# Queries of the narrow-headed cross attention made tile by tile amid its steps, and rooms for returned rows allotted first

## The chip, the cores and the metric

The kernel runs on one core of one Trainium2 chip. The metric is the device time of one execution in microseconds, as the median of several runs. The page and the trace come from one profiled execution. Its engines are PE (matrix products, with PEld for its weight loads), DVE (vector), ACT (scalar), POOL (GpSimd) and SP, which here issues DMAs. "PEclk" or "granted clock" is the share of full speed that PE's clock had.

## The reference, cut to what matters

A network of four levels works on x, 16 batches of 64 rows of 256 numbers (1024 rows, 8 tiles of 128), with a context of 16 x 1024 rows of 192. Every level adds a cross attention to the context, an attention of some kind and an expert or dense layer. All numbers are f32. The change touches the cross attention of level 1 and, at its edge, the expert layer of level 0 ahead of it:

```python
# L0_ffn: 8 experts, two for each row
y = sum over e of comb[:, e] * swiglu(x_e, w1[e], w2[e], w3[e])   # + a shared swiglu
# L1_xattn: 16 heads of 16, on the normalised x
q = (x @ Wq.T + bq).reshape(b, l, 16, 16)
kv = (y @ Wkv.T + bkv).reshape(b, m, 16, 32); k, v = kv[..., :16], kv[..., 16:]
att = softmax(einsum('blhd,bmhd->blmh', q, k) / 4, axis=2)
out = einsum('blmh,bmhd->blhd', att, v).reshape(b, l, 256) @ Wo.T + bo
...
x = x + L0_ffn(layernorm(x))
x = x + L1_xattn(layernorm(x), ctx)
```

## The kernel before, in words

One program runs eight stages one after the other: L0_first, L0_ffn, L1_xattn, L1_attn, L1_ffn, L2_xattn_attn, L2_ffn and L3. x stays in SBUF as `xs`, eight tiles of 128 rows by 256. The order of PE's instructions is written out by hand in each stage. The orders of the other engines are set by a scheduler from the same code, so work of a later stage can stand amid that of an earlier one on DVE, ACT and POOL, and PE's order may do so at a stage's edge. Each stage has an SBUF pool (`self.lp`) at one end of memory, with the stages taking turns between the two ends; a tile of a new stage that lies on tiles of an old one waits until those tiles' last readers are done. PSUM of L1_xattn has three banks tagged `misc` (L69), used in turn.

**End of L0_ffn.** Expert results were written to DRAM (`ys`). For each of 8 tiles and each of two experts, `take_back` (L1191) gathers 128 rows by an indirect DMA on POOL's queue (L1189) into a room tagged `back` with three buffers, and DVE adds them, weighed, to `xs` (L1102): 16 gathers and 16 adds.

**L1_xattn** (L782 to L966). It begins by setting up small masks (L795 on) and its tile `qs`, two versions of all queries, 16 KB a partition each: `qs0` as computed and `qs1` with its two halves of 64 partitions exchanged, by DMA (L826). Then, in PE's order:

1. `keys_values(0)` (L830): four pieces, keys(0), values(0), keys(1) and values(1), for batch 0. Keys take four passes of 512 columns over 128 rows (L844) and four over 64 (L846), into two banks that DVE (L849) and ACT (L850) evict with a bias into `kT`. Values take eight passes (L858) and eight (L865), evicted into `v` by DVE (L58) and ACT (L60).
2. `biases()` (L806): the output bias and that of the values as one row of 256, spread over 128 partitions. DVE makes `bv` (L809), PE multiplies, and ACT copies to `bias` (L812).
3. `norm_x()` (L182): normalises all eight tiles. Per tile DVE takes statistics (L152, L154, L156), POOL the power -0.5 (`ln_rs`, L158), DVE writes `htok` (L168), PE transposes twice (L177) and an eviction writes into `hT` (L58 or L60).
4. Eight additions of `bias` to `xs` on POOL (L934).
5. `queries(0)` and `queries(1)` (L814): 16 passes of 512 columns, eight DVE operations of 128x512 (L821) that add a bias and mask the two heads of a pair, and four DMAs of 512 KB.
6. 64 steps (L937 on), four for each batch. A step makes scores (L65, `sc<-kT,qs`, two versions of `qs` for the two halves of keys), on which DVE takes row maxima (L221) and ACT exponentials (L223). Beside them PE does a quarter of the next batch's keys or values, transposes the exponentials of the step before (L233, evicted by DVE at L237 and ACT at L235) and multiplies them by values (L892). Every eight steps a tile's result is weighed, projected and added to `xs` (L85).

Of the kernel before, what the change touches and what calls it, by code (L numbers as in the profile page):

```python
# [10 lines left out]
F32 = mybir.dt.float32  # L11
# [3 lines left out]
ALU = mybir.AluOpType  # L15
# [3 lines left out]
B, S, D = 16, 64, 256  # L19
T = B * S  # L20
NT = T // 128
# [19 lines left out]
class Net:  # L41
# [740 lines left out]
    def L1_xattn(self):  # L782
# [4 lines left out]
        nc = self.nc  # L787
        wq, wk, wv, wo, bo = self.pack()
# [7 lines left out]
        for h in range(2):  # L796
            nc.sync.dma_start(sels[0][32 * h : 32 * h + 8], sel[:, h])
            for half in range(2):
                at = 64 * half
                nc.sync.dma_start(sels[1][32 * h : 32 * h + 8, :, at : at + 64], sel[:, h, :, 64 - at : 128 - at])  # L800

        qs = [self.lp.tile([128, 2, B, 2, S], F32, name=f"qs{n}") for n in range(2)]

        bias = self.lp.tile([128, D], F32, name="bias")

        def biases():  # L806
            bv = self.lp.tile([128, 2, 128], F32, name="bv")
            for c in range(2):
                nc.vector.tensor_scalar(bv[:, c, :], self.ones, self.col("L1x_bv", c), None, ALU.mult)  # L809
            ps = self.misc([128, D])  # L810
            self.mm(ps, [(bv[:, c, :], wo[:, c, :]) for c in range(2)] + [(self.ones[:1, :], bo)])
            nc.scalar.copy(bias, ps)  # L812

        def queries(half):  # L814
            cols = bass.ts(half, 512)
            bs = slice(half * 8, half * 8 + 8)
            for o in range(2):
                ps = self.misc([128, 512])
                self.mm(ps, [(wq[:, c, o * 128 : (o + 1) * 128], self.hT[:, c, cols]) for c in range(2)])
                for h in range(2):  # L820
                    nc.vector.tensor_scalar(  # L821
                        qs[0][:, o, bs, h, :], ps.rearrange("p (b s) -> p b s", s=S),
                        self.col("L1x_bq", o), self.pair4[:, h : h + 1], ALU.add, ALU.mult,
                    )
            for r in range(2):
                nc.sync.dma_start(qs[1][64 * r : 64 * r + 64, :, bs], qs[0][64 - 64 * r : 128 - 64 * r, :, bs])  # L826

        kv = {}

# [44 lines left out]
        def scores(b, g, sums):  # L874
            kT = kv[b][0]
            sc = [self.lps.tile([128, KEYS], F32, tag="sc", bufs=2, name="sc") for _ in range(2)]
            c = g // 2
            for kh in range(2):
                at = bass.ts(kh, 512)
                for u in range(2):  # L880
                    j = (2 * g + u + 2 * kh) % 4
                    rows = slice(32 * j, 32 * j + 32)
                    self.mm(sc[u][:, at], [(qs[kh][rows, c, b].rearrange("p h q -> p (h q)"), kT[rows, c, at])])
            return [self.exp_rows(sc[u], sums[:, 2 * g + u : 2 * g + u + 1]) for u in range(2)]

        def averages(b, g, pT, o):
# [39 lines left out]

        self.room_t = self.misc
        with self.tc.manual_schedule(engines={mybir.EngineType.PE}):
            for piece in keys_values(0):
                piece()  # L930
            biases()
            self.norm_x()
            for i in range(NT):
                nc.gpsimd.tensor_tensor(self.xs[:, i, :], self.xs[:, i, :], bias, ALU.add)  # L934
            for half in range(2):
                queries(half)
            held, work = None, {}  # L937
            steps = [(b, g) for b in range(B) for g in range(4)]
            for k in range(len(steps) + 4):
                now, pT = None, []  # L940
                if held is not None:
                    hb, hg, p, hs = held
                    for u in range(2):
                        pT.append(self.keys_first(p[u]))
                if k < len(steps):
                    b, g = steps[k]
                    if not g:
                        sums = self.lp.tile([128, 8], F32, tag="sums", bufs=3, name="sums")
                        more = keys_values(b + 1) if b + 1 < B else None
                    now = (b, g, scores(b, g, sums), sums)  # L950
                for piece in work.pop((k, "early"), ()):
                    piece()
                if k < len(steps):
                    if more is not None:
                        more[g]()
                if held is not None:
                    if not hg:
                        o = self.lps.tile([128, 2, 2, 128], F32, tag="o", bufs=1, name="o")
                    averages(hb, hg, pT, o)
                for piece in work.pop((k, "late"), ()):  # L960
                    piece()
                if held is not None and hg == 3:
                    i, par = hb // 2, hb % 2
                    if not par:
                        ym = self.lp.tile([128, 2, 2, 2, S], F32, tag="ym", bufs=2, name="ym")
                    own_columns(o, ym, par)  # L966
                    work[k + 1, "early"] = [lambda hs=hs, par=par, rT=rTs[i % 2]: shares(hs, par, rT)]
                    if par:
                        work[k + 2, "early"] = [lambda ym=ym, rT=rTs[i % 2]: weigh(ym, rT)]
                        work[k + 3, "late"] = [lambda i=i, ym=ym: project(i, ym)]  # L970
                held = now
# [83 lines left out]

    def L0_ffn(self):
        nc = self.nc
        p = self.gate_softmax(self.logits)
        masks, both = self.two_largest(p)
        self.scattered = []  # L1060
        place, count = self.ranks(both)
        first, self.rows = self.blocks(count, L0_BLOCKS)
        at, gates = [], []
        for k, m in enumerate(masks):
            at.append(self.slots_of(m, place, first, f"s{k}"))
            self.scatter(at[k], "L0f")
            g = self.gate("g_of")
            nc.vector.tensor_tensor(g, p, m, ALU.mult)
            gates.append(self.over_experts(g, ALU.add, f"g_{k}")[0])
        for _ in self.swiglu(  # L1070
            *self.shared, 384, self.add_to_x, 1, lambda: self.lps.tile([128, 512], F32, tag="gu", bufs=4, name="gu")
        ):
            pass
        self.start_pack(self.at)
        sizes = [128] * 5 + [64]
        for j in range(L0_BLOCKS):
            w13, w2 = self.L0_block(j)
            dT = self.block_tokens(j)
            hid = self.lp.tile([128, 6, 128], F32, tag="hid1", bufs=2, name="hid1")
            for m2 in range(3):  # L1080
                ps = self.lps.tile([128, 2, 2, 128], F32, tag="gu", bufs=4, name="gu")
                for v in range(2):
                    m = m2 * 2 + v
                    n = sizes[m]
                    for u in range(2):
                        self.mm(
                            ps[:n, u, v, :], [(w13[:, u, c, m * 128 : m * 128 + n], dT[:, c, :]) for c in range(2)]
                        )

                for lo, v, n in ((0, 2, 128),) if m2 < 2 else ((0, 1, 128), (1, 1, 64)):  # L1090
                    g = self.lp.tile([128, 2, 128], F32, tag="g1", bufs=3, name="g1")
                    nc.scalar.activation(g[:n, :v, :], ps[:n, 0, lo : lo + v, :], AF.Silu)
                    nc.vector.tensor_tensor(
                        hid[:n, m2 * 2 + lo : m2 * 2 + lo + v, :], g[:n, :v, :], ps[:n, 1, lo : lo + v, :], ALU.mult
                    )
            po = self.lps.tile([128, D], F32, tag="o", bufs=2, name="po")
            self.mm(po, [(hid[:n, m, :], w2[:n, m, :]) for m, n in enumerate(sizes)])
            self.block_out(j, po)
        for i in range(NT):
            for k in range(2):  # L1100
                y = self.take_back(at[k], i)
                nc.vector.scalar_tensor_tensor(  # L1102
                    self.xs[:, i, :], y, gates[k][:, i : i + 1], self.xs[:, i, :], ALU.mult, ALU.add
                )
# [85 lines left out]

    def take_back(self, at, i):  # L1191

        y = self.lp.tile([128, D], F32, tag="back", bufs=3, name="back")
        self.gather_rows(y, self.ys, at[:, i : i + 1])
        return y

    def block_tokens(self, j):

# [28 lines left out]
    def L1_ffn(self):  # L1227
        nc = self.nc
        rw, rb, b2 = self.pack()
        self.norm_x()  # L1230
        p = self.gate_softmax(self.gate_logits(rw, rb))
        mask = self.first_largest(p, "t1")
# [16 lines left out]
        for j in range(L1_BLOCKS):  # L1249
# [3 lines left out]
            for m4 in range(2):  # L1253
                ph = self.lps.tile([128, 4, 128], F32, tag="h", bufs=3, name="ph")
                for u in range(4):
                    m = m4 * 4 + u
# [26 lines left out]
    def L2_ffn(self):  # L1283
        nc = self.nc
        gw, gb = self.pack()
        self.norm_x()
        lg = self.gate("lg")
        nc.vector.tensor_copy(lg, self.gate_logits(gw, gb))
# [903 lines left out]
```

## Time and profile before

| what | us |
|---|---|
| runs | 3138.62, 3132.53, 3132.1 |
| median | 3132.53 |
| profiled execution | 3130.54 |
| its span in the trace | 3128.8 |
| first gather of returned rows, start | 542.11 |
| last L1102 add, start | 570.83 |
| PE's first pass after it (keys(1) of batch 0) | 572.20 |
| first half of scores of step 0 | 592.04 |
| second half of scores of step 0 | 597.48 |
| scores of step 1 | 607.11 |
| scores of step 2 | 614.26 |

The span is 1.7 us shorter than the profiled execution that it belongs to, and that execution is 2 us shorter than the median of the runs. Times of the table's lower part count from the span's start. A step's length can be read from the last two rows: 7.15 us. In the stretches of the profile, a row gives an interval, its length, then for each engine the busy time with its instruction count in brackets, the granted clock, the DMA engines' mean busy share and GB/s. In a timeline, brackets at the end of a line give the idle time of that engine just before and what ended it.

### The profile page before, as it was taken

What the parts mean: (1) busy time and instruction counts of PE and PEld (TensorE: products, weight loads), DVE (VectorE), ACT (ScalarE), POOL (GpSimd) and SP (SyncE); (2) the same over time, 40 slices, a digit from 0 to 9 for tenths busy, and PEclk for the clock granted to TensorE, in tenths of its full rate; (3) what the DMA queues carried; (4) which work ended last, traced back from release to release, by engine and by line L of the source; (5) the groups of instructions that cost most, each with busy time, mean ns of one, the idle gap of its engine ahead of it and who ended that gap; (6) DMA issues with size and microseconds to landing.
All of it is one profiled execution on the core that took longest, in us unless ns stands there. A gap on an engine that the chain in (4) does not pass through costs nothing.

```text
span 3128.8 us, 42567 instructions
## 1 busy us (share of the span) xinstructions
PE 2750.3 (88%) x16976; PEld 1987.6 (64%) x16976; DVE 1463.2 (47%) x2986; ACT 1010.6 (32%) x2160; POOL 310.5 (10%) x425
## 2 busy tenths in 40 slices
PE   6887899699999879788999999496999888887899
PEld 3654787366666536675777776494777566665668
DVE  2553111566666672124444443322345656658591
ACT  1221121255555411122322332021225445455330
POOL 1112221200000010320011000202000000000000
PEclk9897899799999988799999999698999999998999
DMA  9612774201010100761211111373113212122110
GB/s 231 187 41 73 276 275 179 60 31 32 21 32 23 47 1 27 271 217 35 60 42 41 52 51 51 126 248 112 51 41 87 70 41 88 47 72 58 52 37 7
DMA packets 149408, 273.18 MB, mean 87 GB/s; under 512 B 16511, under 2 KB 103258, under 8 KB 142426
## 3 DMA queue, kind: packets, MB, share of 16 engines
q1 hardware_dynamic: 127418, 170.90, 18.6%
q0 software_dynamic: 14784, 93.26, 8.3%
q10 hardware_dynamic: 7008, 6.29, 0.6%
q8 instruction: 134, 2.20, 0.3%
q14 instruction: 64, 0.52, 0.1%
HBM read 247.83 MB, written 20.45 MB: 86 GB/s over the span
## 4 chain that ended last, share of the span: by engine, by line
PE 65%; DVE 10%; issue 7%; ACT 4%; DMA 3%; POOL 2%; SPq 1%; ACTq 0%; DVEq 0%; POOLq 0%
PE misc L65 10%; PE sc L498 8%; PE halves L65 7%; PE gu L65 6%; PE po L65 4%; PE misc L233 4%; PE ps_h L65 4%; PE ps_t L233 3%; PE sc L65 2%; PE misc L844 2%; PE o L892 2%; PE misc L858 2%; DVE x L1832 2%; ACT p L223 2%; PE misc L177 2%
## 5 line engine op out<-in xcount | busy, mean ns | idle before, releaser
L221 DVE TENSOR_REDUCE nmx<-sc 128x1 f32<-128x1024 f32 x264 | 311.7, 1219 | 243.9 <-PE sc L498 148.1
L223 ACT ACTIVATE p<-sc,nmx 128x1024 f32<-128x1024 f32 x264 | 294.0, 1115 | 323.7 <-DVE nmx L221 322.4
L498 PE MATMUL sc<-ctxT,qp 128*128 128x512 f32 (+1 forms) x1024 | 353.9, 600 | 0.0
L498 PEld LDWEIGHTS sc<-ctxT,qp 128*128 128x128 f32 (+1 forms) x1024 | 138.2, 189 | 153.4 <-issue 151.9
L158 POOL TENSOR_TENSOR ln_rs<-ln_ve,nhalf 128x1 f32<-128x1 f32 x120 | 66.7, 561 | 1531.3 <-DVE ln_ve L156 1267.0
L65 PE MATMUL halves<-ctx,pT 128*128 128x193 f32 x1024 | 189.3, 339 | 9.2 <-DVE xs L85 4.1
L65 PEld LDWEIGHTS halves<-ctx,pT 128*128 128x128 f32 x1024 | 177.2, 200 | 12.0 <-DVE xs L85 4.6
L65 PE MATMUL misc<-ctx,pT 128*128 128x193 f32 x1024 | 179.3, 327 | 0.9 <-DVE qT L463 0.9
L65 PEld LDWEIGHTS misc<-ctx,pT 128*128 128x128 f32 x1024 | 167.7, 191 | 2.8 <-DVE qT L463 1.6
L233 PE MATMUL ps_t<-ident,p 128*128 128x128 f32 x1088 | 148.0, 279 | 18.1 <-ACT p L223 10.5
L1832 DVE TENSOR_TENSOR_SCAN x<-da,x 128x512 f32<-128x512 f32 x128 | 152.2, 1213 | 2.1 <-ACT da L1822 1.4
L235 ACT COPY pT<-ps_t 128x512 f32<-128x512 f32 x182 | 103.8, 582 | 149.0 <-PE ps_t L233 148.6
L1822 ACT ACTIVATE da<-rep,al 128x252 f32<-128x252 f32 x256 | 114.8, 498 | 111.1 <-DVE x L1832 90.2
L233 PEld LDWEIGHTS ps_t<-ident,p 128*128 128x128 f32 x1088 | 128.2, 144 | 32.1 <-ACT p L223 13.4
L233 PE MATMUL misc<-ident,p 128*128 128x128 f32 x1024 | 136.8, 279 | 7.1 <-ACT p L223 6.7
L65 PE MATMUL gu<-dT,wa 128*128 128x128 f32 (+1 forms) x1104 | 133.5, 280 | 4.0 <-issue 3.5
L65 PEld LDWEIGHTS gu<-dT,wa 128*128 128x128 f32 (+1 forms) x1104 | 125.7, 185 | 12.7 <-ACT yb L1207 6.3
L233 PEld LDWEIGHTS misc<-ident,p 128*128 128x128 f32 x1024 | 110.1, 141 | 32.7 <-ACT p L223 13.6
L65 PE MATMUL po<-wb,hid 128*128 128x256 f32 x516 | 124.5, 388 | 0.0
L65 PE MATMUL ps_h<-r,w 128*128 128x256 f32 x512 | 115.3, 385 | 0.0
L65 PEld LDWEIGHTS ps_h<-r,w 128*128 128x128 f32 x512 | 97.8, 192 | 16.6 <-issue 2.9
L237 DVE COPY pT<-misc 128x512 f32<-128x512 f32 x128 | 88.2, 689 | 42.5 <-PE misc L233 36.7
(446 smaller groups left out, 4374.7 us busy)
## 6 DMA issues: line engine op xcount, KB each, us to landing
ctx<-in_ctx SPq DMA_DIRECT2D x48, 768.0 KB
ctxT<-in_ctxT SPq DMA_DIRECT2D x48, 512.0 KB
w<-in_L2f_W SPq DMA_DIRECT2D x24, 1024.0 KB
rep<-dus SPq DMA_DIRECT2D x256, 64.0 KB
ctxT<-in_ctxT SPq DMA_DIRECT2D x16, 768.0 KB
ctxT<-in_ctxT SPq DMA_DIRECT2D x96, 128.0 KB
hb<-hs SPq DMA_DIRECT2D x46, 128.0 KB
ys<-yb ACTq DMA_DIRECT2D x46, 128.0 KB
```

The source lines that it names most:

```text
L65: self.nc.tensor.matmul(out, lhsT, rhs, start=n == 0, stop=n == len(pairs) - 1)
L158: nc.gpsimd.tensor_tensor(rs, ve, self.nhalf, ALU.pow)
L177: self.nc.tensor.transpose(ps[:, c, :], o[:, c * 128 : (c + 1) * 128], self.ident)
L221: self.nc.vector.tensor_reduce(nmx, sc, AX.X, ALU.max, negate=True)
L223: self.nc.scalar.activation(p, sc, AF.Exp, bias=nmx, accum_out=sums)
L233: self.nc.tensor.transpose(ps[:, u, :], p[:, at : at + 128], self.ident)
L235: self.nc.scalar.copy(pT[:, 4 * g : 4 * g + 4, :], ps)
L237: self.nc.vector.tensor_copy(pT[:, 0:4, :], ps)
L498: nc.tensor.matmul(sc[u][:, bass.ts(kh, 512)], qp[n][par][rows, h : h + 2, :].rearrange("p h q -> p (h q)"), ctx[0][rows, at], start=n == ...
L844: nc.tensor.matmul(ps[kh], wk[:, kh, cols], cT[:, bass.ts(kh, 512)], start=True, stop=False)
L1822: nc.scalar.activation(da[:, g, :, 1:], now[j][:, 0, :].rearrange("p (b s) -> p b s", s=S)[:, :, 1:], AF.Exp, scale=al[:, col : col + 1],)
L1832: nc.vector.tensor_tensor_scan(flat, da.rearrange("p g b s -> p (g b s)"), flat, 0.0, ALU.mult, ALU.add)
```

## The change: what it does

In L1_xattn, `biases()` moves ahead of `keys_values(0)`. `norm_x()`, the eight additions in one place and the two halves of `queries` go. A generator `queries(i)` for one tile of 128 rows takes their place, in three parts: normalise tile i and add `bias` to `xs` of that tile; transpose and evict into an `hT` of 128 columns; eight passes of 128 columns into one `misc` bank, four DVE operations, and two DMAs of 128 KB. Tiles 0 and 1 are done before the steps. Tiles 2 to 7 follow, one part in each of the first three steps of every even batch, two tiles ahead of their use. `qs` of a tile takes 2 KB a partition and version, with three buffers.

In the expert layers, three rooms `back0` to `back2` are allotted by `rooms_back()` as the first tiles of the stage and used in turn, where `take_back` had taken a tagged tile with three buffers at the end of the stage. `rooms_back()` is called at the beginning of L0_ffn, and after `pack()` in L1_ffn and L2_ffn.

```diff
-        qs = [self.lp.tile([128, 2, B, 2, S], F32, name=f"qs{n}") for n in range(2)]
...
-        def queries(half):
...
+        qs = {}
+        def queries(i):
+            mv, rs = self.norm_tile(self.xs[:, i, :], 1e-5)
+            o = self.lp.tile([128, D], F32, tag="o", bufs=2, name="o")
+            nc.vector.tensor_scalar(o, self.xs[:, i, :], mv[:, 0:1], rs, ALU.subtract, ALU.mult)
+            nc.gpsimd.tensor_tensor(self.xs[:, i, :], self.xs[:, i, :], bias, ALU.add)
+            yield
+            hT = self.lp.tile([128, 2, 128], F32, tag="hT", bufs=2, name="hT")
+            self.evict(hT, self.transposed(o))
+            yield
+            ps = self.misc([128, 2, 128])
+            for m in range(2):
+                self.mm(ps[:, m, :], [(wq[:, c, m * 128 : (m + 1) * 128], hT[:, c, :]) for c in range(2)])
+            qs[i] = [self.lp.tile([128, 2, 2, 2, S], F32, tag=f"qs{n}", bufs=3, name=f"qs{n}") for n in range(2)]
+            for m in range(2):
                 for h in range(2):
                     nc.vector.tensor_scalar(
...
+                        qs[i][0][:, m, :, h, :], ps[:, m, :].rearrange("p (b s) -> p b s", s=S),
+                        self.col("L1x_bq", m), self.pair4[:, h : h + 1], ALU.add, ALU.mult,
                     )
             for r in range(2):
+                nc.sync.dma_start(qs[i][1][64 * r : 64 * r + 64], qs[i][0][64 - 64 * r : 128 - 64 * r])
+            yield
...
         with self.tc.manual_schedule(engines={mybir.EngineType.PE}):
+            biases()
             for piece in keys_values(0):
                 piece()
-            biases()
-            self.norm_x()
-            for i in range(NT):
-                nc.gpsimd.tensor_tensor(self.xs[:, i, :], self.xs[:, i, :], bias, ALU.add)
-            for half in range(2):
-                queries(half)
+            for i in range(2):
+                for _ in queries(i):
+                    pass
...
                 if k < len(steps):
+                    if not b % 2 and not g and b // 2 + 2 < NT:
+                        ahead = queries(b // 2 + 2)
                     if more is not None:
                         more[g]()
+                    if b % 2 == 0 and g < 3 and b // 2 + 2 < NT:
+                        next(ahead)
...
     def take_back(self, at, i):
-        y = self.lp.tile([128, D], F32, tag="back", bufs=3, name="back")
-        self.gather_rows(y, self.ys, at[:, i : i + 1])
-        return y
+        self.backs.append(self.backs.pop(0))
+        self.gather_rows(self.backs[-1], self.ys, at[:, i : i + 1])
+        return self.backs[-1]
+
+    def rooms_back(self):
+        self.backs = [self.lp.tile([128, D], F32, name=f"back{n}") for n in range(3)]
```

More of the change, by code (lines that the diff above doesn't have):

```diff
@@ L812, in biases @@
             nc.scalar.copy(bias, ps)
-        def queries(half):
[L815 to L819, printed above, removed]
+        qs = {}
[13 more added lines that the diff above has]
+            for m in range(2):
                 for h in range(2):
                     nc.vector.tensor_scalar(
-                        qs[0][:, o, bs, h, :], ps.rearrange("p (b s) -> p b s", s=S),
-                        self.col("L1x_bq", o), self.pair4[:, h : h + 1], ALU.add, ALU.mult,
+                        qs[i][0][:, m, :, h, :], ps[:, m, :].rearrange("p (b s) -> p b s", s=S),
+                        self.col("L1x_bq", m), self.pair4[:, h : h + 1], ALU.add, ALU.mult,
                     )
             for r in range(2):
-                nc.sync.dma_start(qs[1][64 * r : 64 * r + 64, :, bs], qs[0][64 - 64 * r : 128 - 64 * r, :, bs])
+                nc.sync.dma_start(qs[i][1][64 * r : 64 * r + 64], qs[i][0][64 - 64 * r : 128 - 64 * r])
+            yield
         kv = {}
@@ L882, in scores @@
                     rows = slice(32 * j, 32 * j + 32)
-                    self.mm(sc[u][:, at], [(qs[kh][rows, c, b].rearrange("p h q -> p (h q)"), kT[rows, c, at])])
+                    self.mm(
+                        sc[u][:, at],
+                        [(qs[b // 2][kh][rows, c, b % 2].rearrange("p h q -> p (h q)"), kT[rows, c, at])],
+                    )
             return [self.exp_rows(sc[u], sums[:, 2 * g + u : 2 * g + u + 1]) for u in range(2)]
@@ L1057, in L0_ffn @@
         nc = self.nc
+        self.rooms_back()
         p = self.gate_softmax(self.logits)
@@ L1229, in L1_ffn @@
         rw, rb, b2 = self.pack()
+        self.rooms_back()
         self.norm_x()
@@ L1285, in L2_ffn @@
         gw, gb = self.pack()
+        self.rooms_back()
         self.norm_x()
```

## The prediction

> **What bounds the kernel now.** I first read the page's first part: PE is busy for 88% of the span, DVE for 47%. A whole-span share says nothing on one stage, so I next cut the stage that the diff rewrites, L1_xattn, into stretches (columns: busy time and instructions of PE, PEld, DVE, ACT, POOL, then the granted clock, DMA share and GB/s).
>
> ```profile
> PE 2750.3 (88%) x16976; PEld 1987.6 (64%) x16976; DVE 1463.2 (47%) x2986; ACT 1010.6 (32%) x2160; POOL 310.5 (10%) x425
> ```
> ```profile
> 560.00:572.00 12.00, 0.00 (x0) 0.00 (x0) 7.88 (x24) 0.00 (x0) 7.98 (x14) 0.50 0.22 64
> ...
> 592.00:598.00 6.00, 1.69 (x7) 0.80 (x8) 1.53 (x2) 0.00 (x0) 0.00 (x0) 0.95 0.99 223
> 598.00:607.00 9.00, 8.74 (x28) 3.39 (x24) 3.92 (x5) 3.61 (x6) 0.00 (x0) 0.66 0.36 74
> ...
> 640.00:700.00 60.00, 60.00 (x567) 37.68 (x568) 39.05 (x52) 32.85 (x61) 0.55 (x1) 1.00 0.09 28
> ```
>
> There are two regimes. Until 607 us PE stands still or runs at a lowered clock; from there to about 1060 it is busy for all of the time at clock 1.00. Work taken out of the first regime is won only if the wait that ends last is shortened; each us of PE work put into the second costs a us. The timeline of PE tells what ends the waits (start, duration, then idle time and releaser in brackets):
>
> ```profile
> 572.20 3.78 PE L844 MATMUL misc<-ctxT,w 128*128 128x512 f32 x4 [26.64 <-DVE kT L849]
> ...
> 582.59 2.51 PE L177 MATMUL misc<-ident,htok 128*128 128x128 f32 x16
> 584.98 7.13 PE L65 MATMUL misc<-hT,w 128*128 128x512 f32 x16
> 592.04 1.13 PE L65 MATMUL sc<-kT,qs 32*128 32x512 f32 x4
> 597.48 2.07 PE L65 MATMUL sc<-kT,qs 32*128 32x512 f32 x4 [4.31 <-DMA qs<-qs]
> 599.49 3.78 PE L844 MATMUL misc<-ctxT,w 128*128 128x512 f32 x4
> ```
>
> PE waits 26.64 us for the first key eviction on DVE (L849), at 571.41. That was not slow: on DVE it is queued behind L0_ffn's 16 adds of rows given back (L1102) and seven normalises (L168). Then 4.31 us go to the DMA that copies the queries with halves swapped (4 x 512 KB, the last issued at 595). After it a group of four key passes takes 3.78 us, against 1.98 at 539.08 with a warm clock. POOL and DVE ahead of it:
>
> ```profile
> 542.11 0.95 POOL L1189 DMA_INDIRECT back<-ys,s_at  x1 [29.68 <-issue]
> 543.36 0.95 POOL L1189 DMA_INDIRECT back<-ys,s_at  x1 [0.30 <-issue]
> ```
> ```profile
> 562.16 0.99 POOL L1189 DMA_INDIRECT back<-ys,s_at  x1 [1.13 <-DVE xs L1102]
> ...
> 567.24 0.99 POOL L1189 DMA_INDIRECT back<-ys,s_at  x1 [0.18 <-issue]
> ```
> ```profile
> 569.83 1.08 DVE L168 TENSOR_SCALAR htok<-xs,ln_mv,ln_rs 128x256 f32<-128x256 f32 x1 [0.75 <-POOL ln_rs L158]
> 570.83 0.47 DVE L1102 SCALAR_TENSOR_TENSOR xs<-back,g,xs 128x256 f32<-128x256 f32 x1
> ```
>
> The reader is to see the pitch of gathers, 1.25 us when nothing is in their way, and that it is lost later: a gather waits for an add to free its room, the add stands on DVE behind a normalise, and the normalise waits for POOL's `ln_rs`, which stands between gathers.
>
> **Part 1, rows given back (gathers end earlier).** The rooms become first tiles, so they lie on the lowest addresses of the right-hand pool, where L1_xattn's `bv` and first `kT` will lie. All work that writes those must wait until the last add has read its room. In engine order the change also takes norms of tiles 2 to 7 out of the stretch: DVE has no normalise between adds, POOL about four `ln_rs` (0.57) before the last gather. Last gather: 542.11 + 15 x 1.25 + 4 x 0.5 = 562.9; it lands 2.8 later (542.11 to the add at 544.91), and an add is 0.48: 566.2 against 571.30. I take **5.1 us**. Bounds: 0 if the chain keeps its pace, 7 if no `ln_rs` is in the way. Pitch holds with three rooms: 2.8 + 0.48 = 3.28 is under 3 x 1.25 = 3.75, a slack of only 0.47.
>
> What is lost: before, keys and values (first pieces, 539.08 to 545.56) ran under the gathers. Now `biases()` is first on PE, needs `bv`, and so all waits for the last add. In L0_ffn, L1_ffn and L2_ffn the rest of the order is the same; rooms elsewhere cost 0.
>
> **Part 2, the way to the first scores.** PE from 566.5 (`bv` is two DVE operations of 0.27): biases 1.69, four pieces 2 x 6.48 = 12.96 (539.08 to 545.56 is one pair), cold start 2.22 (the pair at 572.20 took 8.70 rather than 6.48), small waits 0.3: 583.7. Tile 0: two transposes 0.3, eviction on ACT behind that of values 1.0, eight passes of 128 columns 0.95 (48 of that form took 5.72 at 530.44). Tile 1 adds 1.85 (DVE: four query operations 1.4, one `hT` 0.42) and 0.95: 588.6, first half of scores. Four issues of 128 KB rather than 512 KB: the last about 588, landing 2 later (before, 597.48 is 1.6 after the end of the last issue, 595.9), so the second half starts at **590.1**, against 597.48: 7.4 won, although 6.5 us of covered work became uncovered. The rest of that sum is seven tiles' query passes and the long DMA, which no longer stand here.
>
> **Part 3, the clock.** Before, the pass after the 4.31 wait runs at 0.50 and it takes 9.63 us from 597.48 to the scores of step 1 (607.11). Warm: scores 1.1, keys 1.98 + 1.13, then transposes bound by exp: 1.1 + one reduce of 1.22 + two exps of 1.30 + eight transposes of 0.13 = 5.96, with two hand-overs 6.05. So 3.6 more, **11.0** in all, if the clock stays. In the row 592 to 598 an idle PE of 4.31 was enough; the new gaps are 1 to 1.9 each. But a low clock also follows stretches with a little work:
>
> ```profile
> 1084.00:1088.00 4.00, 1.37 (x8) 0.66 (x7) 3.90 (x17) 0.37 (x1) 1.09 (x2) 1.00 1.04 388
> 1088.00:1092.00 4.00, 1.43 (x6) 0.78 (x6) 3.43 (x15) 0.00 (x0) 1.40 (x3) 0.61 0.18 56
> ```
>
> Here PE was busy for a third of the time, and the clock fell. From 583.7 to 590.1 PE is busy for about 3 of 6.4. I take warm, as it is nearer to the half-busy side; the other end is the 3.6 given back, and 0.6 more for slow query passes.
>
> [...]
>
> **Part 4, six tiles amid the steps.** Per tile: two transposes 0.13 each (16 in 2.08 inside a step), eight passes 0.12 each: 1.22 us, on a PE that has no idle time: 6 x 1.22 = **7.3 us paid**. Bounds: 0 if PE has hidden slack (1000 to 1060 shows 57.60 of 60.00 busy), 8.1 at 0.135 a pass (a step's passes with 40 rows). The rest is covered: DVE gets per tile a norm of 1.2, half of an eviction 0.42, four operations of 0.41 (`hp<-misc`, same shape): 3.1 in some 21 us of three steps, where it is busy for 39.05 of 60; ACT 32.85 of 60; POOL nearly idle; SP has two issues of 128 KB that stand two batches (57 us) ahead of their use. Each insertion borrows one of three `misc` banks, and its readers are DVE or ACT: as DVE has some 35% idle, I set the wait at 0, up to 1 us per insertion with a 1.22 reduce ahead of it.
>
> **Sum.** -5.1 (gathers) and -2.3 (rest of the way to 590.1) and -3.6 (clock) make -11.0; +7.3 in the steps: **-3.7 us**. Against the profiled execution (3130.54, span 3128.8) that is 3126.8; the median of the runs is 3132.53, 2 above the profiled one, and by it 3128.8. I state 3128.5. What follows (L1_attn on) starts earlier by as much, since PE, not a DMA, sets its start.
>
> **Rivals.**
> - A, the clock falls in the query phase (583 to 590): -11.0 + 4.2 + 7.3 = +0.5, 3131 to 3133. For it: the 1088 row. Against: PE half busy.
> - B, the insertions cost more than their passes. Place: the 12 bank users in the steps (transposes, passes). Price: w us of PE wait each. Sign turns at w = 3.7 / 12 = 0.31; with w = 1, +12 - 3.7 = +8.3: 3139 to 3141, slower. For it: three banks only, and PE without slack. Against: all of PE 60.00 of 60.00 with the same banks today, DVE a third idle.
> - C, gathers are no faster (an `ln_rs` or a room in the way each time): +5.1, so +1.4: 3132 to 3134. For it: the slack of 0.47. Against: no normalise among adds.
> - D, the insertions go into slack that a modelled PE hides: with half of 7.3 free and the clock kept, -7.4 to -11: 3119.5 to 3125. For it: PE's busy time is modelled, 57.60 of 60.00 late in the stage. Against: 60.00 of 60.00 early.
>
> **How the numbers follow.** A measurement tells about 0.2%, 6.3 us, from no change: below 3126.2 is faster, above 3138.8 slower. Base 0.42, A 0.17, B 0.10, C 0.08, D 0.23. Faster: D nearly whole (0.21) and the base's lower part, where its terms lie 2.6 better (0.16): 0.37. Slower: B's upper part and A or C with some of B's wait: 0.11. Same: 0.52. The base's own range is 3125 to 3131. The full range takes in most of D, A, C and B's lower part: 3120.5 to 3137.5; B's upper part and D's end are left out.
>
> **What would show it.** Right: the last L1102 add ends near 566; PE's first L1_xattn work after it; second half of scores near 590 with clock 1.00 until 600; scores of step 1 near 596; from there the gain shrinks by 1.2 us per two batches until step 42. Wrong: low clock in 588 to 600 (A); PE idle after `hT` or `qs` groups inside steps (B); gathers waiting for adds (C); fewer than 7 us lost between step 1 and step 42 (D). Wrong altogether would be a shift outside L1_xattn, above all at the other two expert layers.

## The result, and the profile after

Over 12 runs of each, the changed kernel took 3131.97 us (median, 3128.04 to 3143.66) and the kernel before 3132.63 us (3124.51 to 3138.62). The ratio is 1.0008 with a 95% interval of 0.9998 to 1.0019: no change that can be told. The profiled execution of the changed kernel took 3130.77 us (span 3129.0), that of before 3130.54 (3128.8).

So a prologue was rebuilt and six tiles' work moved, and nothing came of it in the total. The traces say where it went. As the first gather of returned rows starts at 542.11 in one execution and at 538.74 in the other (the stages ahead of it are the same, and over the profiled executions of this study it started anywhere from 533.4 to 556.4), the times below count from the start of that first gather ("from G").

PE's timeline in the changed kernel, L1_xattn's start (start, duration, at the end the idle time before it and what ended that):

```profile
563.75 2.07 PE L65 MATMUL misc<-w,bv 128*128 128x256 f32 x4 [27.96 <-DVE bv L807]
...
566.90 3.54 PE L854 MATMUL misc<-ctxT,w 128*128 128x512 f32 x4
...
581.33 0.44 PE L177 MATMUL misc<-ident,o 128*128 128x128 f32 x2
582.35 1.16 PE L65 MATMUL misc<-hT,w 128*128 128x128 f32 x8 [0.58 <-ACT hT L60]
583.34 0.38 PE L177 MATMUL misc<-ident,o 128*128 128x128 f32 x2
585.29 1.16 PE L65 MATMUL misc<-hT,w 128*128 128x128 f32 x8 [1.57 <-DVE hT L58]
586.38 3.56 PE L65 MATMUL sc<-kT,qs 32*128 32x512 f32 x8
589.87 3.78 PE L854 MATMUL misc<-ctxT,w 128*128 128x512 f32 x4
...
597.18 1.14 PE L65 MATMUL sc<-kT,qs 32*128 32x512 f32 x8
```

The reader is to see three things. The long wait is still there, 27.96 us, now ahead of the biases. The sixteen passes of 512 columns and the wait of 4.31 us for the DMA are gone. But the four key passes at 589.87 take 3.78 us, as long as those at 599.49 before, and the eight score passes at 586.38 take 3.56 us where the next eight, at 597.18, take 1.14. The stretches show why (busy PE, PEld, DVE, ACT, POOL, granted clock, DMA share, GB/s):

```profile
583.72:587.13 3.41, 1.84 (x13) 1.27 (x12) 2.81 (x10) 0.00 (x0) 1.31 (x3) 1.00 0.43 114
587.13:590.55 3.42, 3.31 (x7) 1.00 (x6) 1.31 (x4) 0.00 (x0) 0.00 (x0) 0.50 0.40 89
```

PE was busy for 1.84 of 3.41 us, without any gap above 1.6, and then the clock fell to half. The gathers and adds, on POOL and DVE:

```profile
558.66 0.95 POOL L1205 DMA_INDIRECT back<-ys,s_at  x1 [0.31 <-issue]
559.99 0.94 POOL L1205 DMA_INDIRECT back<-ys,s_at  x1 [0.38 <-DVE xs L1118]
```
```profile
562.83 0.48 DVE L1118 SCALAR_TENSOR_TENSOR xs<-back,g,xs 128x256 f32<-128x256 f32 x1 [1.00 <-DMA back<-ys,s_at]
```

Apart from the four `ln_rs` operations between them, gathers keep a pitch of 1.25 to 1.33 us to the end: the last one starts 21.25 us from G (25.13 before). The last add starts at 562.83, 24.09 from G, against 28.72 before. Then the steps. A stretch early in the steps of the changed kernel has PE busy for all of its time, as before:

```profile
640.00:700.00 60.00, 60.00 (x545) 37.78 (x543) 40.40 (x57) 31.35 (x58) 1.28 (x2) 1.00 0.11 32
```

and in it stand the inserted groups, with no idle time around them:

```profile
600.17 1.13 PE L875 MATMUL misc<-w,ctxT 64*128 64x256 f32 x8
601.24 0.44 PE L177 MATMUL misc<-ident,o 128*128 128x128 f32 x2
601.61 1.08 PE L905 MATMUL o<-pT,v 128*32 128x128 f32 x32
...
608.75 1.16 PE L65 MATMUL misc<-hT,w 128*128 128x128 f32 x8
609.83 1.08 PE L905 MATMUL o<-pT,v 128*32 128x128 f32 x32
```

From one start to the next: 0.37 us for two transposes, 1.08 for eight passes. The ledger, in us from G (maxima are the first DVE reduce of a step):

| | before | changed | difference |
|---|---|---|---|
| end of the last add | 29.19 | 24.58 | -4.6 |
| second half of scores of step 0 | 55.38 | 49.12 | -6.3 |
| maxima of step 1 | 66.22 | 59.65 | -6.6 |
| maxima of step 44 | 389.79 | 392.12 | +2.3 |
| maxima of step 63, the last | 528.24 | 531.94 | +3.7 |

6.6 us are won ahead of the steps and 8.9 paid in them, and 1.4 more are lost at their end, where the clock fell once at 1054.8 in the changed kernel and not in the one before.

### The profile page after: what moved, and what is told of

Read it like the earlier page. It is cut to its first block, busy times and chain, and to the rows that moved or that the text cites. A ratio compares the mean times of both kernels' runs of the same rounds, so it can differ in the third digit from the quotient of the medians.

```text
span 3129.0 us, 42702 instructions
## 1 busy us (share of the span) xinstructions
PE 2751.3 (88%) x17024; PEld 1989.3 (64%) x17024; DVE 1466.8 (47%) x3010; ACT 1010.9 (32%) x2160; POOL 311.4 (10%) x425
## 4 chain that ended last, share of the span: by engine, by line
PE 41%; DVE 8%; ACT 3%; DMA 3%; issue 2%; POOL 2%; SPq 1%; ACTq 0%; DVEq 0%; POOLq 0%
PE sc L498 8%; PE misc L65 8%; PE halves L65 7%; PE ps_h L65 4%; PE ps_t L233 3%; PE po L65 3%; PE gu L65 2%; PE ph L65 2%; DVE x L1854 2%; PE halves L1878 2%; ACT p L223 1%; DVE nmx L221 1%; DVE x L1850 1%; DMA rep<-dus 1%; PE misc L177 1%
## 5 line engine op out<-in xcount | busy, mean ns | idle before, releaser
L235 ACT COPY pT<-misc 128x512 f32<-128x512 f32 x128 | 75.0, 586 | 107.6 <-PE misc L233 107.3
```

Source lines behind the costliest of these rows:

```text
L235: self.nc.scalar.copy(pT[:, 4 * g : 4 * g + 4, :], ps)
```

## The experiments

**The theory (T):** the start of L1_xattn is set by the queue of DVE, in which everything of that stage stands behind the adds; the changed kernel wins what it takes out of that queue and out of the query phase, loses the same low clock as before, and pays for each inserted tile's PE work in full. **Rivals:** that the rooms' new place makes PE wait (R), that insertions cost waits for banks rather than passes (B), that the clock is not what is lost. Each run below was also timed beside the kernel before.

| run | maxima of step 1, from G | step 1 to 44 | last step, from G | ratio to before (95%) |
|---|---|---|---|---|
| before | 66.22 | 323.57 | 528.24 | |
| changed | 59.65 | 332.47 | 531.94 | 1.0008 (0.9998 to 1.0019) |
| e1 rooms only | 66.21 | 323.48 | 528.14 | 1.0008 (0.9992 to 1.0023) |
| e2 queries only | 59.67 | 332.45 | 531.95 | 1.0015 (1.0001 to 1.0029) |
| e3 clock filled | 56.85 | 332.44 | 529.13 | 1.0023 (1.0010 to 1.0037) |
| e5 passes twice | 59.67 | 337.83 | 535.95 | 1.0043 (1.0028 to 1.0058) |
| e6 ACT evicts, rooms last | 52.39 | 332.43 | 525.18 | 0.9975 (0.9960 to 0.9990) |
| e7 ACT evicts, rooms first | 59.96 | 332.81 | 532.63 | 1.0010 (0.9996 to 1.0024) |
| e8 before, ACT evicts | 59.46 | 323.53 | 521.45 | 0.9984 (0.9972 to 0.9995) |
| e9 queries under gathers | 57.94 | 326.41 | 522.80 | 0.9987 (0.9976 to 0.9999) |
| e10 the same, p first | 41.16 | 326.51 | 507.57 | 0.9954 (0.9932 to 0.9976) |
| e11 as e6, p first | 46.68 | 332.45 | 517.92 | 0.9971 (0.9957 to 0.9985) |
| e12 six tiles first | 70.96 | 326.85 | 536.24 | 1.0028 (1.0014 to 1.0042) |

**e1, one part alone: the rooms.** The kernel before, with `rooms_back()` and the new `take_back`.

> The kernel before with one part of the change alone: the three rooms for returned rows as first tiles of each expert layer. Theory T (the queries' move is all that counts, the rooms cost and bring nothing): from the start of the first gather to the end of the last L1102-type add 29.2 us, to the maxima of step 1 66.2 us, both as before within 0.7, and the total within 0.2% of before. Rival R (the rooms lie under tiles that L1_xattn writes first, so keys and values wait for the last add): the keys of batch 0 no longer start within 1 us of the last expert block, and step 1 comes 5 to 7 us later, 71 to 73.

Every mark lies within 0.1 us of before, up to the last step. By the addresses of the built program, which no view here shows, the rooms lie under `qs` in this kernel, and `qs` is written only after all tiles are normalised. T holds, R falls for this half of the change.

**e2, the other part alone: the queries.** The changed kernel with the old `take_back`.

> The changed kernel with the rooms allotted at the end of the stage again, as before. Theory T: as the changed kernel within 0.7, i.e. 24.6 us from the first gather to the end of the last add, about 48 to the first scores and 59.7 to the maxima of step 1, because the pass that begins L1_xattn waits for two DVE operations that stand behind all adds, wherever the rooms lie. Rival R (the rooms force that wait): PE begins the biases under the gathers, and step 1 comes at 45 to 50.

Within 0.02 us of the changed kernel at every mark of the table, with a wait of 28.01 us for `bv`. So the 27.96 us of waiting for `bv` in the changed kernel are not due to the rooms. `bv` needs no returned row: its two DVE operations stand in DVE's order behind all sixteen adds, whether the rooms are under it or not.

**e3, the clock.** Idle gaps of the query phase are filled with transposes that nobody reads:

```diff
-            self.evict(hT, self.transposed(o))
+            ot = self.transposed(o)
+            self.evict(hT, ot)
+            if i < 2:
+                idle = self.misc([128, 2, 128])
+                for n in range(4 + 10 * i):
+                    nc.tensor.transpose(idle[:, n % 2, :], o[:, :128], self.ident)
```

> The changed kernel with PE kept busy in the query phase ahead of the steps: 4 extra transposes after those of tile 0 and 14 after those of tile 1, into a bank that nobody reads. Theory T (the low clock at the first scores costs 3.4 us): the clock stays at 1.00 from the warm-up to step 1, the maxima of step 1 come at 56 to 57 us after the first gather rather than 59.7, and the steps from there on are as in the changed kernel (332.5 from step 1 to step 44). Rival (the clock is not what is lost, the waits for evictions and the DMA are): step 1 at 59 to 60 or later.

PE's timeline in e3 at the same place:

```profile
585.08 1.69 PE L827 MATMUL misc<-ident,o 128*128 128x128 f32 x14
586.81 1.16 PE L65 MATMUL misc<-hT,w 128*128 128x128 f32 x8
587.90 1.13 PE L65 MATMUL sc<-kT,qs 32*128 32x512 f32 x4
589.39 1.13 PE L65 MATMUL sc<-kT,qs 32*128 32x512 f32 x4 [0.36 <-DMA qs<-qs]
590.45 1.98 PE L859 MATMUL misc<-ctxT,w 128*128 128x512 f32 x4
```

The clock is 1.00 from 581 to 602 there. The same passes take 1.98 us rather than 3.78, step 1 comes at 56.85 rather than 59.65, and from second scores to those of step 1 it takes 6.41 us (589.39 to 595.80). The clock's price at this place, 2.8 us, is shown. But the total did not follow: e3 is 1.0023 of before. In its profiled execution, the part behind the maxima of step 63 takes 2064.8 us, against 2058.3 in the changed kernel. At the edge from L1_ffn to the next stage, stretches of the changed kernel and then of e3:

```profile
1412.00:1420.00 8.00, 4.73 (x20) 4.09 (x20) 5.90 (x24) 2.06 (x4) 3.24 (x6) 0.50 0.04 14
1420.00:1428.00 8.00, 6.95 (x44) 4.19 (x46) 1.68 (x6) 2.94 (x6) 0.00 (x0) 1.00 0.01 2
```
```profile
1412.00:1420.00 8.00, 4.15 (x19) 3.81 (x20) 5.87 (x25) 2.06 (x4) 4.12 (x6) 0.50 0.05 17
1420.00:1428.00 8.00, 6.28 (x37) 4.98 (x37) 2.31 (x6) 1.99 (x6) 0.00 (x0) 0.50 0.01 2
```

The code is the same there, yet one ran at clock 1.00 from 1420 on and the other at 0.50 until 1428. That the 2.8 us were handed back because later gaps fall differently on the changes of clock is argued, not shown. e2, whose steps end within 0.02 us of the changed kernel's, takes 2054.9 us for the same part, so single executions differ by several us there even when the steps end alike.

**e5, the insertions' price.** The eight query passes of the six inserted tiles are made twice, into the same bank:

```diff
-            for m in range(2):
+            for m in (0, 1) * (1 if i < 2 else 2):
                 self.mm(ps[:, m, :], [(wq[:, c, m * 128 : (m + 1) * 128], hT[:, c, :]) for c in range(2)])
```

> The changed kernel with the eight query passes of each of the six tiles amid the steps made twice into the same bank. Theory T (the steps pay for the passes themselves, 0.135 us each): 332.5 + 6 x 1.08 = 339.0 us from step 1 to step 44. Rival B (what an insertion costs is the wait for a bank or for the queue of DVE, in which passes hide): under 335.5.

337.83, that is 5.36 for 48 more passes, 0.112 each: T's side, with a smaller size than the 0.135 of T. In the trace of e5 the group of sixteen takes 1.98 us from its start to the next (614.32 to 616.30), where the group of eight took 1.08, so the second eight cost 0.90. Nothing hid in waits. B falls.

**e6 and e7, DVE's queue taken away, and the rooms' place once more.** The changed kernel with ACT in DVE's place for batch 0; e6 has the rooms at the end as before, e7 as first tiles:

```diff
-                nc.vector.tensor_scalar(bv[:, c, :], self.ones, self.col("L1x_bv", c), None, ALU.mult)
+                nc.scalar.activation(bv[:, c, :], self.zero[:, :128], AF.Identity, bias=self.col("L1x_bv", c))
...
-                nc.vector.tensor_scalar(kT[:, o, :512], ps[0], self.col("L1x_bk", o), None, ALU.add)
+                if b:
+                    nc.vector.tensor_scalar(kT[:, o, :512], ps[0], self.col("L1x_bk", o), None, ALU.add)
+                else:
+                    nc.scalar.activation(kT[:, o, :512], ps[0], AF.Identity, bias=self.col("L1x_bk", o))
...
-                    self.evict(v[:, 4 * kh + 2 * s : 4 * kh + 2 * s + 2, :], ps[kh])
+                    put = self.evict if b else nc.scalar.copy
+                    put(v[:, 4 * kh + 2 * s : 4 * kh + 2 * s + 2, :], ps[kh])
```

> The changed kernel with rooms at the end of the stage as before, and with ACT instead of DVE making the two bias tiles bv and evicting the keys and values of batch 0. Theory T (what PE waits for at the start of L1_xattn is DVE's queue of adds, not the data): PE makes biases, keys and values under the gathers, the last add still ends at 24.6 us after the first gather, the first scores come at 32 to 36 rather than 47.6, and the maxima of step 1 at 42 to 47 rather than 59.7; the steps are unchanged (332.5 from step 1 to 44). Total some 12 us under the changed kernel. Rival (PE waits for something else that ends with the adds): no change, 59 to 60.

> As the run before it, but with the rooms as first tiles, as in the change. Theory T2 (the rooms of the change lie under the first tiles of L1_xattn, which hides behind DVE's queue in the changed kernel and shows once that is gone): PE waits for the last add again, first scores at 46 to 49, step 1 at 58 to 61, some 15 us later than with rooms at the end. Rival (the rooms cost nothing wherever they lie): within 1 us of the run with rooms at the end.

e6: PE's first passes no longer wait, but the next do (PE, then ACT):

```profile
531.75 1.13 PE L65 MATMUL misc<-w,bv 128*128 128x256 f32 x4 [1.26 <-ACT bv L807]
...
558.86 2.93 PE L871 MATMUL misc<-w,ctxT 128*128 128x256 f32 x6 [21.75 <-ACT kT L862]
```
```profile
558.12 0.69 ACT L862 ACTIVATE kT<-misc,vecs 128x512 f32<-128x512 f32 x1 [24.21 <-DVE xs L1121]
```

So half of what T expected came (52.39; 42 to 47 was expected): behind the queue of DVE stood a second wait, that of ACT's first `kT` eviction, which reads no returned row and yet starts only after the last add (L1121). e7 has the whole 28 us back (28.13 us at `bv`, now released by ACT, which itself waits for the last add), step 1 is 7.6 us later than in e6, and the total 1.0010 against 0.9975:

```profile
568.90 0.69 ACT L807 ACTIVATE bv<-zero,vecs 128x128 f32<-128x128 f32 x2 [27.26 <-DVE xs L1122]
```

So the rooms' new place does have a price, which the queue of DVE hid in the changed kernel. T2's mechanism is right; its 15 us were twice what was measured, as e6 had a wait of its own.

**e8, the same edit on the kernel before.**

> The kernel before with ACT instead of DVE making bv and evicting the keys and values of batch 0, nothing else. Theory T: keys(1), values(1) and biases move under the gathers; last add at 29.2 as before; then 16 transposes and 16 passes of 512 columns, at a low clock at first, so first scores at 43 to 47 rather than 49.9, second half still behind the DMA of queries, step 1 at 57 to 62 rather than 66.2; steps 323.5. Rival: no change, 66.2.

Step 1 at 59.46, as far as the whole change brought it, and with no insertions to pay: 323.53. With nothing but ACT in DVE's place it begins the steps as early as the changed kernel, and it is a little faster than before (0.9984, with an interval that ends at 0.9995).

**e9 and e10, queries under the gathers.** The kernel of e8, with queries tile by tile, six tiles ahead of the steps and two in batches 8 and 10. Normalised and transposed rows lie in the tiles that `norm_x` used, and ACT evicts queries:

```diff
+        def queries(i):
+            mv, rs = self.norm_tile(self.xs[:, i, :], 1e-5)
+            nc.vector.tensor_scalar(self.htok[:, i, :], self.xs[:, i, :], mv[:, 0:1], rs, ALU.subtract, ALU.mult)
+            yield
...
+                    nc.scalar.activation(
+                        qs[0][:, m, bs, h, :], ps[:, m, :].rearrange("p (b s) -> p b s", s=S), AF.Identity,
+                        bias=bqp[:, m, h : h + 1], scale=self.pair4[:, h : h + 1],
+                    )
```

> A version that takes the waits away: the kernel before with ACT evictions for batch 0, and queries tile by tile, six tiles under the gathers (normalised rows and transposed rows in the tiles of norm_x, queries evicted by ACT with scale and bias), the last two amid the steps of batches 8 and 10. If the theory of DVE's queue holds, PE works while rows are given back: first scores at 28 to 33, step 1 at 38 to 43 rather than 66.2 (before) or 59.7 (changed), steps 323.5 + 2 x 1.48 = 326.5, total some 20 to 25 us under before, ratio 0.992 to 0.994. Rival: ACT or the DMAs of queries become the bound, step 1 at 50 or later.

The expectation failed: step 1 at 57.94, and 0.9987 in the total where 0.992 to 0.994 was expected. PE made keys, values, biases and one tile, and then stood until the last add (PE, then ACT):

```profile
568.01 2.08 PE L65 MATMUL misc<-hT,w 128*128 128x128 f32 x8 [17.08 <-ACT hT L826]
```
```profile
566.19 1.51 ACT L834 ACTIVATE qs<-misc,w,pair 128x128 f32<-128x128 f32 x4 [17.01 <-DVE xs L1126]
```

ACT's queue was held by its first query eviction, which waited for the last add (L1126). By the addresses in the built programs, which no view here shows, `qs` lay on the small tiles of L0_ffn with the rows' indices and weights, which every gather and every add reads, and so did the first `kT` of e6. e10 puts `p`, first written in step 0, on that place, and moves the mask DMAs to POOL's queue; e11 below makes the first of these two edits alone, in e6:

```diff
+        self.lp.tile([128, KEYS], F32, tag="p", bufs=2, name="p")
         qs = [self.lp.tile([128, 2, B, 2, S], F32, name=f"qs{n}") for n in range(2)]
...
-            nc.sync.dma_start(sels[0][32 * h : 32 * h + 8], sel[:, h])
+                nc.gpsimd.dma_start(sels[0][32 * h : 32 * h + 8], sel[:, h])
```

> The version with queries under the gathers (e9) once more, with two edits: the tile p, first written in step 0, is allotted ahead of the queries, so that queries, keys and values no longer lie on the index and weight tiles that the gathers and adds read to the end; and the mask DMAs go to POOL's queue. Theory (in e9 ACT's first query eviction waited for the last add, because its tile lay on those): ACT evicts tile 0's queries at 12 to 14 us after the first gather, PE works between the gathers, first scores by 30 us, step 1 at 38 to 43 rather than 57.9, total 13 to 18 us under e9. Rival (ACT waits for the adds by another chain): step 1 stays at 57 to 58.

```profile
550.43 1.16 PE L65 MATMUL misc<-hT,w 128*128 128x128 f32 x8 [0.46 <-ACT bias L810]
...
568.29 2.08 PE L65 MATMUL misc<-hT,w 128*128 128x128 f32 x8 [1.44 <-ACT hT L822]
570.29 2.09 PE L65 MATMUL sc<-kT,qs 32*128 32x512 f32 x8
```
```profile
538.00:562.00 24.00, 18.75 (x87) 12.24 (x86) 11.16 (x34) 11.31 (x27) 17.18 (x20) 0.88 0.50 136
```

ACT evicts tile 0's queries at 551.62, 13.48 from G (12 to 14 was expected), where e9 came to it at 29.24. PE is busy for 18.75 of the 24 us from 538 on; in the kernel before it was for 3.27 of the 24 us from its first gather on. The first scores come at 32.16 from G (30 was expected), step 1 at 41.16, within what was expected, and the total is 0.9954 of before, 3114.41 us against 3132.19 (medians): 12.6 us under e9's median, a little short of the 13 to 18 that were expected. This version beats both kernels.

**e11, the same trap taken out of e6.** One line, `p` ahead of the other tiles.

> e6 (changed kernel, rooms last, ACT evictions for batch 0) with one edit: the tile p is allotted ahead of the others, so that the first kT no longer lies on the index and weight tiles of the last gathers and adds. Theory: PE makes all keys and values of batch 0 under the gathers instead of standing for 21.75 us at the second bank, first scores at 31 to 36 rather than 43.7, step 1 at 42 to 47 rather than 52.4. Rival (the ACT wait was on something else): 52 to 53 again.

46.68: PE makes all keys and values under the gathers and then waits 12.42 us for the first normalised tile (`DVE o`). As this is e6 with one line more, the place of the tiles is shown to be the cause of the 21.75 us; which old tiles lay there is known from the addresses alone. The total, 0.9971, does not differ from e6's beyond the intervals, although the last step comes 7.3 us earlier.

**e12, the trade itself.** Six tiles ahead of the steps in the changed kernel, two amid them.

> The changed kernel with six tiles ahead of the steps and only two (6 and 7) amid them. Theory T (an insertion costs 1.48 us in the steps; ahead of the steps a tile costs its PE work and the wait for its evictions, 2.5 to 3 us): from step 1 to step 44 323.5 + 2 x 1.48 = 326.5 us rather than 332.5; first scores 10 to 12 us later than 47.6, so 58 to 60; in sum 4 to 6 us slower than the changed kernel at the last step. Rival (a tile ahead of the steps is cheaper than one amid them): first scores under 53, last step earlier than 531.9.

Four insertions fewer save 5.62 us (332.47 to 326.85, 1.41 each), and first scores come 13.6 later (61.27; 58 to 60 was expected). That is 3.4 us a tile, with passes that had slowed by then: the eight of the third tile take 2.08 us, those of the first 1.16. The last step is 4.3 later, and the total 1.0028. Amid the steps is the cheaper place, as long as the tiles ahead stand alone on the path.

## Why the prediction was right or wrong

- **Gathers (-5.1):** measured -4.6. The mechanism, that no normalise stands among the adds and so the pitch of gathers holds, was right: the last one started 21.25 us from G, where 20.8 was forecast.
- **"All work that writes those must wait until the last add has read its room":** the wait was there, its cause was another. e2 has it without the rooms under `bv`: it was DVE's order. The rooms' cost is real only where that queue is gone (e6 against e7, 7.6 us). In the sum it made no difference.
- **Way to the second scores (-7.4, with the gathers in it):** measured -6.3. From the end of the last add it took 24.5 us, where 23.9 was forecast and 26.2 had been spent before.
- **"I take warm" (-3.6):** this step failed. From second scores to those of step 1 it took 9.32 us, where 6.05 were forecast and 9.62 had been spent before: 0.3 of the 3.6 us was won. e3 has clock 1.00 from 581 to 602 and takes 6.41. The prediction chose warm because PE would be about half busy there; it was, for 1.84 of 3.41 us, and the clock fell all the same, to 0.50. That the clock would stay, and with it the 3.6, was the author's estimate, and no run shows it with PE half busy in the query phase; in e3, where step 1 came 2.8 us earlier, PE was busy for 3.37 of the 3.41 us from 584.50 on.
- **Insertions (+7.3):** measured +8.9, above the upper bound of 8.1. All six are paid, as forecast (e5), but each is 1.45 to 1.48 rather than 1.22: the row of 48 passes in one group (0.12 each) was the wrong one for a group of eight (1.08 in all), and two transposes by themselves take 0.37, not 0.26. The price of 0.135 a pass, taken for the bound, was that of these passes.
- **Sum (-3.7):** with the measured terms, -6.6 + 8.9 = +2.3 at step 44. That is rival A's course (+0.5) with the insertions 1.6 dearer. The forecast time, 3128.5, lies 3.5 under the measured median, and the likeliest outcome, a change within 0.2%, is what came. That is in part luck: the sign of the sum was wrong, and the measured median lies in rival A's 3131 to 3133, above the base's own 3125 to 3131. The stated range holds it because it took in A.
- **"What follows (L1_attn on) starts earlier by as much":** this failed too, unnoticed by the total: the steps ended 3.7 us later, and the part behind them took 2058.3 us as against 2058.4 before. Over the thirteen profiled executions that part took between 2054.9 and 2064.8 us. e3 was 2.8 us ahead of the changed kernel at the last step and no faster in the total. The ratios of all runs follow the last step within some 6 us.
- **B, C, D:** no waits for banks (e5), gathers were faster, and no slack under PE in the steps.

Open stays why e3 and e5 are slower than their last step says, and why e11 gains no more than e6; no run held the clock in the later stages.

## What to carry to other kernels

A wait that ends with a chain of small operations may have three causes one behind another: the order of an engine's queue (27.96 us in the changed kernel), then an address shared with a tile that the chain still reads (21.75 in e6), and only then the data (12.42 in e11). Each had to be taken away here before the next one showed. Moving work to an idle engine brought step 1 forward by as much (e8, 6.8 us) as rebuilding the prologue did (6.6), and together with freed addresses and queries under the gathers by 25.1 (e10). Work moved into stretches where PE had no idle time was paid at the price of short groups (1.45 to 1.48 us a tile), so take that price from a short group. Where PE is half busy, price both clocks: in the changed kernel a stretch with 1.84 of 3.41 us busy was followed by clock 0.50 and one with 1.79 by 1.00.

## What was not expected of the hardware

- The clock fell after a stretch in which PE was busy for 1.84 of 3.41 us. At the end of the steps one stretch of 1.39 was followed by a fall and one of 1.79 by none, in the changed kernel:

```profile
1051.34:1054.76 3.42, 1.39 (x34) 1.12 (x27) 3.38 (x5) 1.90 (x3) 0.00 (x0) 1.00 0.00 0
1054.76:1058.17 3.41, 3.41 (x19) 2.43 (x18) 1.42 (x3) 1.61 (x4) 0.00 (x0) 0.50 0.00 0
1065.00:1068.41 3.41, 1.79 (x36) 1.30 (x26) 2.44 (x3) 2.33 (x4) 0.00 (x0) 1.00 0.00 0
```

  So busy time alone does not settle it: the stretch with 1.84 was followed by a fall and that with 1.79 was not. In the kernel before, a stretch of 3.41 us without any PE work (from 593.95) was followed by a fall to 0.50, and one with 1.79 of 3.42 us (from 1051.33) by none; in e3 one with 3.37 of 3.41 (from 584.50) was followed by none. What decides it between those is not shown.
- Within L1_xattn, two profiled executions of the same code there agree to a tenth of a microsecond (maxima of the last step at 528.24 in before and 528.14 in e1, at 531.94 in the changed kernel and 531.95 in e2, from the first gather), while the totals of the changed kernel's twelve runs spread by 15.6 us.
